# Sparse graph attention on one core: slot sums as accumulating float32 transposes, a count read one step later, and other FFN chunks

## The chip, the core and the metric

One Trainium2 chip, one of its eight cores. A core has five engines that run their own instruction streams in program order and meet at semaphores: TensorE (PE, with its weight loads PEld), VectorE (DVE), ScalarE (ACT), GpSimd (POOL) and SyncE (SP). DMA engines move data between the memory of the chip (HBM) and the on-chip memory (SBUF); TensorE writes its results to PSUM. The metric is the device time of the whole program in microseconds; less is better.

## What is computed

Four graph layers on 3327 nodes with 256 features, and an adjacency matrix in which an entry is set with probability 0.0048, some 16 neighbours for a node. Layer 0 is a one-head attention. Layers 1 to 3 are transformer layers with 8 heads of 32 features, in which a node attends to its neighbours only:

```python
def layer(x, adj, w_qkv, w_proj, b_proj, w1, b1, w2, b2, g1, be1, g2, be2):
    qkv = layer_norm(x, g1, be1) @ w_qkv              # float32 throughout
    q, k, v = split(qkv)                              # n x 8 heads x 32
    scores = einsum('nhd,mhd->hnm', q, k) * 32 ** -0.5
    scores = where(adj != 0, scores, -inf)
    attn = softmax(scores)
    out = einsum('hnm,mhd->nhd', attn, v).reshape(n, 256)
    x = x + out @ w_proj + b_proj
    ff = gelu(layer_norm(x, g2, be2) @ w1 + b1) @ w2 + b2      # 256 -> 1024 -> 256
    return x + ff
```

## The kernel before

Stage one computes layer 0 with dense products of the turned adjacency matrix. It also makes, for each node, the list of its neighbours, sorts the nodes by their number of neighbours and cuts them into 26 blocks of 128 nodes. A block `b` needs as many slots as its longest list has entries:

```python
CAPS = [40, 24, 22, 21, 20, 20, 19, 19, 18, 18, 17, 17, 17,
        16, 16, 15, 15, 15, 14, 14, 13, 13, 12, 12, 11, 10]      # 448 slots in all
GS = 4          # slots of one group: gathered into one buffer, worked on together
NBUF = 10       # such buffers
CB = 4          # blocks of one FFN chunk
```

A layer takes the blocks in the order 25, 1, 24, 2, ..., 13, 0. For each slot, POOL issues one gather that fetches the row with keys and values (512 numbers) of one neighbour for each of 128 nodes:

```python
for s in range(n):                                   # in issue(): n = 4 slots, or what is left
    nc.gpsimd.indirect_dma_start(out=t[:, s, :], in_=kv[L], in_offset=...neighbour s of block b...)
```

DVE multiplies the keys by the queries and sums over each head (`scores`, L1320 and L1321), and later multiplies the values by the softmax weights (L1361). PE then sums the slots: a product with the identity leaves each number as it is and PSUM adds it up. Slots are taken two at a time, so that even and odd slots land in two halves of a PSUM bank:

```python
nc.vector.tensor_mul(vw..., v, weights...)                                    # L1361
for s in range(0, n, 2):
    m = min(2, n - s) * D
    nc.tensor.matmul(self.po[b][:, :m], ident, vw[:, s * D:s * D + m],        # L1366
                     start=(s0 + s == 0), stop=(s0 + s + 2 >= S), skip_group_check=True)
self.issue()            # the buffer is free: gather the next group into it
```

When a block's slots are summed, a short list of steps is worked off, up to two steps in each turn; an empty step lets one half turn pass:

```python
def copy():    nc.scalar.copy(c["o"], self.po[b][:, :D])                      # L1384, even slots
def fold():    nc.vector.tensor_add(c["o"], c["o"], self.po[b][:, D:])        # L1387, + odd slots
def turn():                                                                   # L1391
    for k in range(2):
        nc.tensor.transpose(self.po[b][:, k * P:(k + 1) * P], c["o"][:, k * P:(k + 1) * P], ident)
def copy_T():  nc.scalar.copy(c["oT"], self.po[b][:, :2 * P])                 # L1396
def project(): ...  # bias (L1400) and c["oT"] @ w_proj (L1402), into the other half of po
def add():     ...  # x += po (L1406), and the moments for the norm
return [lambda: None, copy, lambda: None, fold, turn, copy_T, project, lambda: None, add]
```

Two blocks at most can own an accumulator `po` at a time. After the last block of a chunk, the norm, the FFN and (in layers 1 and 2) the next layer's q, k and v of these blocks become a long list of steps (`up` L1445, `gelu` L1451, `down` L1468, `back` L1482, `qkv` L1498), which is spread over the turns of the four blocks that follow. Every turn has one group's scores, one group's values and some of these steps.

In stage one, for every four blocks, a step `soft` marks the number of neighbours of each node (`OH`) and has PE count, with products of triangular matrices, the place of each node among the nodes with as many neighbours; DVE reads the count at once. A step `mix`, half a step of the pipeline later, finishes the weights of layer 0:

```python
def soft(self):
    nc.vector.tensor_tensor(OH[:, b0:b0 + n, :], ..., ALU.is_equal)           # L892
    for j in range(n):
        ...nc.tensor.matmul(at[:, j, :], lhsT, OH[:, m, :], ...)              # L903, 120 in all
    nc.vector.tensor_mul(t, at[:, :n, :], OH[:, b0:b0 + n, :])                # L906, waits for L903
    nc.vector.tensor_reduce(rank[:, b0:b0 + n], t, AX.X, ALU.add)
    ...                                # twelve small DVE steps and two exponentials on ACT
def mix(self):
    ...                                # ten DVE steps
```

Cuts are marked with `...`; the line numbers (L1366) are those of the kernel before.

Of the kernel before, what the change touches and what calls it, by code (L numbers as in the profile page):

```python
# [8 lines left out]
FP = mybir.dt.float32  # L9
# [3 lines left out]
ALU = mybir.AluOpType  # L13
AX = mybir.AxisListType
# [3 lines left out]
P = 128  # L18
N = 3327
D = 256  # L20
# [12 lines left out]
NB = (N + P - 1) // P  # L33
# [27 lines left out]
CB = 4  # L61
# [462 lines left out]
def sparse_path(ctx, tc, ins, out, dram, flag):  # L524
    nc = tc.nc
# [3 lines left out]
    ident = const.tile([P, P], FP, name="s_ident")  # L529
# [9 lines left out]
    rank = const.tile([P, NB], FP, name="rank")  # L539
# [83 lines left out]
    with tc.tile_pool(name="a", bufs=1) as a, tc.tile_pool(name="aw", bufs=2) as aw, \  # L623
# [44 lines left out]
        o = 0  # L668
        for name, n in (("gamma", D), ("beta", D), ("bt", H0), ("Wa", H0), ("ba", 1)):
# [10 lines left out]
        nd = LMAX + 1  # L680
# [3 lines left out]
        OH = a.tile([P, NB, nd], BF, name="OH")  # L684
        rest_tri = a.tile([P, P], BF, name="rest_tri")
        nc.vector.tensor_sub(rest_tri, ones_bf, tri)

        places = a_acc.tile([P, 512], FP, tag="places", name="places")
# [3 lines left out]
                         skip_group_check=True)  # L692
# [148 lines left out]
        class Group:  # L841
# [36 lines left out]
            def soft(self):  # L878


                g, n, b0 = self.g, self.n, self.blocks[0]

                def sv(name):
                    t = aw.tile([P, 4], FP, tag="s_" + name, bufs=1, name=f"s_{name}_{g}")
                    return t[:, :n]

                sg = S.s[:, b0:b0 + n]
                dg = deg[:, b0:b0 + n]
                nc.vector.tensor_copy(dg, self.acc[:, :n, H0])
                top = sv("top")  # L890
                nc.vector.tensor_scalar(top, dg, float(LMAX), None, ALU.min)
                nc.vector.tensor_tensor(OH[:, b0:b0 + n, :],  # L892
                                        num[:, None, :nd].to_broadcast([P, n, nd]),
                                        top[:, :, None].to_broadcast([P, n, nd]), ALU.is_equal)

                at = places[:, :4 * nd].rearrange("p (b k) -> p b k", k=nd)
                for j in range(n):
                    i = b0 + j
                    add = [(tri, i)] + [(ones_bf, k) for k in range(b0, i)]
                    if g:  # L900
                        add += [(rest_tri, i - 4)] + [(ones_bf, k) for k in range(i - 3, b0)]
                    for lhsT, m in add:
                        nc.tensor.matmul(at[:, j, :], lhsT, OH[:, m, :], start=False, stop=True,  # L903
                                         skip_group_check=True)
                t = aw.tile([P, 4, nd], FP, tag="place", bufs=1, name=f"place_{g}")[:, :n]
                nc.vector.tensor_mul(t, at[:, :n, :], OH[:, b0:b0 + n, :])  # L906
                nc.vector.tensor_reduce(rank[:, b0:b0 + n], t, AX.X, ALU.add)
                if b0 + n == NB:
                    nc.tensor.matmul(at[:, n - 1, :], rest_tri, OH[:, NB - 1, :], start=False,
                                     stop=True, skip_group_check=True)  # L910
                    S.all = at[:, n - 1, :]
                non, ga, fa, m1, m0, tt, mx = (
                    sv(k) for k in ("non", "ga", "fa", "m1", "m0", "tt", "mx"))
                nc.vector.tensor_scalar(non, dg, -1.0, float(N), ALU.mult, ALU.add)
                nc.vector.tensor_scalar(ga, dg, 0.0, None, ALU.is_gt)
                nc.vector.tensor_scalar(fa, non, 0.0, None, ALU.is_gt)
                nc.vector.tensor_scalar(tt, ga, -NEG0, NEG0, ALU.mult, ALU.add)
                nc.vector.tensor_mul(m1, sg, ga)
                nc.vector.tensor_add(m1, m1, tt)
                nc.vector.tensor_scalar(tt, fa, -1.0, 1.0, ALU.mult, ALU.add)  # L920
                nc.vector.tensor_mul(m0, sg, tt)
                nc.vector.scalar_tensor_tensor(m0, fa, NEG0, m0, ALU.mult, ALU.add)
                nc.vector.tensor_max(mx, m1, m0)
                nc.vector.tensor_sub(m1, m1, mx)
                nc.vector.tensor_sub(m0, m0, mx)
                nc.scalar.activation(m1, m1, AF.Exp)
                nc.scalar.activation(m0, m0, AF.Exp)
                self.non, self.m1, self.m0, self.tt = non, m1, m0, tt

            def mix(self):  # L930
                g, n, b0, acc = self.g, self.n, self.blocks[0], self.acc
                m1, m0, tt = self.m1, self.m0, self.tt
                z = aw.tile([P, 4], FP, tag="s_z", bufs=1, name=f"s_z_{g}")[:, :n]
                nc.vector.tensor_mul(z, deg[:, b0:b0 + n], m1)
                nc.vector.tensor_mul(tt, self.non, m0)
                nc.vector.tensor_add(z, z, tt)
                nc.vector.reciprocal(z, z)
                nc.vector.tensor_mul(m1, m1, z)
                nc.vector.tensor_mul(m0, m0, z)
                shape = [P, n, H0]  # L940
                nb = self.nb = aw.tile([P, 4, H0], FP, tag="nb", bufs=1, name=f"s_nb_{g}")[:, :n]
                t3 = aw.tile([P, 4, H0], FP, tag="t3", bufs=1, name=f"s_t3_{g}")[:, :n]
                nc.vector.tensor_sub(t3, S.hsum[:, None, :].to_broadcast(shape), acc[:, :n, :H0])
                nc.vector.tensor_mul(t3, t3, m0[:, :, None].to_broadcast(shape))
                nc.vector.tensor_mul(nb, acc[:, :n, :H0], m1[:, :, None].to_broadcast(shape))
                nc.vector.tensor_add(nb, nb, t3)

            def project(self):
                g, n = self.g, self.n
# [131 lines left out]
        for g in reversed(range(NG)):  # L1081
            at = dict(zip(names, (0, 1, 3, 4, 5, 6, 7, 8, 9, 10, 11, 12)))
# [11 lines left out]
            for name in names:  # L1094
                k = first + at[name]
# [39 lines left out]
        t = aw.tile([P, NB, nd], FP, tag="v", name="t_more")  # L1135
# [36 lines left out]
        for i in range(NB):  # L1172
            nc.tensor.matmul(pp[:, :2 * NB], oh_lo[:, i, :],
                             ids[:, i, :, :].rearrange("p a b -> p (a b)"),
                             start=(i == 0), stop=(i == NB - 1))
# [32 lines left out]
    work = ctx.enter_context(tc.tile_pool(name="b_work", bufs=2))  # L1208
# [53 lines left out]

    ORDER = [b for k in range(NB // 2) for b in (NB - 1 - k, k + 1)][:NB - 1] + [0]
    CHUNK, at = {}, 0
    for n in [CB - 1] + [CB] * ((NB - CB - 2) // CB) + [2, 1]:
        for b in ORDER[at:at + n]:
            CHUNK[b] = ORDER[at:at + n]
        at += n
# [3 lines left out]
    class Layer:  # L1272
# [77 lines left out]
        def values(self, b, s0):  # L1350

            L, S = self.L, CAPS[b]
            n = min(GS, S - s0)
            t = self.tiles.pop((b, s0))
            if s0 == 0:
                while len(self.po) > 1:
                    self.short.pop(0)()
                self.po[b] = ps_o.tile([P, 512], FP, tag="o", name=f"po_{L}_{b}")
            v = t[:, :n, D:2 * D].rearrange("p s (h d) -> p s h d", d=HD)
            vw = work.tile([P, GS * D], FP, tag="vw", bufs=3, name=f"vw_{L}_{b}_{s0}")  # L1360
            nc.vector.tensor_mul(  # L1361
                vw[:, :n * D].rearrange("p (s h d) -> p s h d", h=HEADS, d=HD), v,
                self.wp[b][:, s0:s0 + n, :, None].to_broadcast([P, n, HEADS, HD]))
            for s in range(0, n, 2):
                m = min(2, n - s) * D
                nc.tensor.matmul(self.po[b][:, :m], ident, vw[:, s * D:s * D + m],  # L1366
                                 start=(s0 + s == 0), stop=(s0 + s + 2 >= S),
                                 skip_group_check=True)
            self.issue()
            if s0 + GS >= S:  # L1370
                self.short += self.block(b)


        def block(self, b):
            L, w, c = self.L, self.w, {}
# [2 lines left out]
            if b == chunk[0]:  # L1378
                self.n2 = Norm(len(chunk), f"f{L}_{b}")
            n2 = self.n2  # L1380

            def copy():
                c["o"] = work.tile([P, D], FP, tag="o", name=f"o_{L}_{b}")
                nc.scalar.copy(c["o"], self.po[b][:, :D])  # L1384

            def fold():
                nc.vector.tensor_add(c["o"], c["o"], self.po[b][:, D:])  # L1387

            def turn():
                for k in range(2):  # L1390
                    nc.tensor.transpose(self.po[b][:, k * P:(k + 1) * P],  # L1391
                                        c["o"][:, k * P:(k + 1) * P], ident)

            def copy_T():
                c["oT"] = work.tile([P, 2 * P], FP, tag="oT", name=f"oT_{L}_{b}")
# [9 lines left out]
            def add():  # L1405
                nc.vector.tensor_add(x, x, self.po.pop(b)[:, D:])  # L1406
                n2.stats(chunk.index(b), x)
                if b == chunk[-1]:
# [3 lines left out]
                    turns = 5 if at == NB - 1 else turns - 2  # L1412
                    self.rate = sum(cost for cost, _ in self.long) / max(turns, 1)

            return [lambda: None, copy, lambda: None, fold, turn, copy_T, project, lambda: None, add]

        def chunk(self, blocks, n2):
            L, w, nxt = self.L, self.w, self.nxt
# [221 lines left out]
```

## Time and profile before

| what | value |
|---|---|
| time, median of 3 timed runs | 3311.32 us (3306.66 to 3313.2) |
| the profiled execution, first to last instruction | 2779.3 us |
| mean granted clock of TensorE in it | 0.836 |
| slot gathers on POOL (L1298) | 1344, 947 ns each, 1272.8 us |
| slot sums on PE (L1366) | 1380 records, 770.4 us |
| DVE on keys (L1320), head sums (L1321), values (L1361) | 413.3, 414.1 and 371.3 us |
| FFN products on PE (L1445, L1468) | 308.1 and 283.4 us |

The profile is of one execution; its span and the timed runs differ, and the page does not say by what. How to read its lines: busy time is the union of an engine's instructions. A group's row gives the line of the kernel, the engine, the operation, the output and the inputs, the shapes, how often it ran, then busy us and mean ns of one, then the idle time of the engine just ahead of these instructions and what ended it. Records of PE overlap, since a matmul starts while the one before it drains, so a group's busy time divided by its count is less than the mean of one. A float32 product shows as two records, each with its weight load. A row of the list of waits reads: who waited, for whom, us in total, times, the longest.

### The profile page before, as it was taken

How to read it: one execution, taken by the hardware profiler on the slowest of the kernel's cores; microseconds unless marked ns; L12 is line 12 of the kernel's file. 1: busy time of each engine (PE TensorE's matmuls, PEld its weight loads, DVE VectorE, ACT ScalarE, POOL GpSimd, SP SyncE). 2: the span in 40 equal slices, each digit the busy share in tenths (PEclk: the TensorE clock that was granted, in tenths of full speed). 3: DMA queues.
4: the chain of work that ended last, by engine and by line, in shares of the span. 5: the costliest groups of instructions: out<-in, count | busy, mean ns of one | idle time of the engine just before them, and what ended most of it. 6: DMA issues, size and time to landing. Idle time of an engine off the chain costs nothing. (4 is left out here: it accounts for less than half of the span.)

```text
span 2779.3 us, 21889 instructions
## 1 busy us (share of the span) xinstructions
PE 1952.0 (70%) x6409; PEld 1045.3 (38%) x6409; DVE 1961.9 (71%) x4061; ACT 806.5 (29%) x1398; POOL 1361.8 (49%) x1458
## 2 busy tenths in 40 slices
PE   5657665248788887884377887887853678867866
PEld 4546553114333333442133443433431333333334
DVE  6597888577877777733788677778427878778852
ACT  5346552102332322321022332232320222222221
POOL 4000000377766666601776565566017777776741
PEclk9768776678899898897788898898976898988988
DMA  6224420677766666613776565566227766666650
GB/s 235 99 106 154 155 81 32 198 217 217 222 196 200 202 182 186 182 34 100 209 211 201 168 195 180 158 190 178 50 70 210 210 183 199 201 190 184 198 130 15
DMA packets 144478, 453.66 MB, mean 163 GB/s; under 512 B 29521, under 2 KB 40156, under 8 KB 141021
## 3 DMA queue, kind: packets, MB, share of 16 engines
q0 software_dynamic: 113056, 370.26, 46.0%
q1 hardware_dynamic: 9834, 53.90, 5.5%
q10 hardware_dynamic: 21458, 28.02, 2.9%
q8 instruction: 52, 0.85, 0.1%
q14 instruction: 78, 0.64, 0.1%
HBM read 420.64 MB, written 31.42 MB: 163 GB/s over the span
## 5 line engine op out<-in xcount | busy, mean ns | idle before, releaser
L1298 POOL DMA_INDIRECT kv<-kv,t x1344 | 1272.8, 947 | 810.0 <-issue 350.4
L1366 PE MATMUL po<-vw,s_ident 128*128 128x512 f32 (+1 forms) x1380 | 770.4, 694 | 497.4 <-DVE vw L1361 447.6
L1320 DVE TENSOR_TENSOR kv<-kv,q 128x1024 f32<-128x1024 f32 (+3 forms) x363 | 413.3, 1139 | 312.6 <-ACT q L1306 156.5
L1366 PEld LDWEIGHTS po<-vw,s_ident 128*128 128x128 f32 x1380 | 285.3, 220 | 846.5 <-issue 468.3
L1321 DVE TENSOR_REDUCE sc<-kv 128x32 f32<-128x1024 f32 (+3 forms) x363 | 414.1, 1141 | 12.4
L1361 DVE TENSOR_TENSOR vw<-kv,w 128x1024 f32<-128x1024 f32 x333 | 371.3, 1127 | 0.2
L1445 PE MATMUL pu<-fT,s_w 128*128 128x512 f32 (+3 forms) x768 | 308.1, 536 | 1.0 <-ACT fT L596 1.0
L1468 PE MATMUL py<-gT,s_w 128*128 128x512 f32 (+2 forms) x672 | 283.4, 549 | 0.0
L1451 ACT ACTIVATE gT<-pu,pvb 128x512 f32<-128x512 f32 (+3 forms) x192 | 116.4, 607 | 361.0 <-PE pu L1445 360.7
L1445 PEld LDWEIGHTS pu<-fT,s_w 128*128 128x128 f32 x768 | 150.6, 206 | 140.5 <-issue 116.0
L711 POOL MEMSET s_abf<- 128x1 bf16 x23 | 2.2, 105 | 375.2 <-DVE s_v L731 248.3
L1468 PEld LDWEIGHTS py<-gT,s_w 128*128 128x128 f32 x672 | 127.6, 191 | 122.0 <-issue 104.4
L723 PE MATMUL s_ptb<-s_ident_bf,s_abf 128*128 128x128 bf16 x676 | 69.8, 273 | 77.3 <-ACT s_abf L714 64.0
L735 DVE MAX8 cand<-s_v 128x8 f32<-128x208 bf16 x416 | 118.0, 359 | 0.9
L588 ACT ACTIVATE xn_f<-t,nm_f,rqy_f 128x256 f32<-128x256 f32 x78 | 42.9, 593 | 247.5 <-DVE nm_f L582 240.1
L1498 PE MATMUL pk<-s_w_qkv,nT 128*128 128x512 f32 x208 | 104.4, 626 | 8.9 <-ACT nT L596 8.9
L1335 ACT ACTIVATE sc<-sc,mx 128x120 f32<-128x120 f32 (+6 forms) x78 | 32.0, 410 | 259.8 <-DVE mx L1332 259.2
L1406 DVE TENSOR_TENSOR t<-t,po 128x256 f32<-128x256 f32 x78 | 32.5, 417 | 103.8 <-PE po L1402 97.9
L1486 DVE TENSOR_TENSOR t<-t,pd 128x256 f32<-128x256 f32 x75 | 29.5, 408 | 91.0 <-PE pd L1482 91.0
L723 PEld LDWEIGHTS <-s_abf 128*128 128x128 bf16 x676 | 58.8, 125 | 91.8 <-ACT s_abf L714 70.8
L855 PE MATMUL s_pa<-s_aT,s_hs 128*128 128x256 bf16 x338 | 80.4, 286 | 13.2 <-DVE s_hs L817 13.2
L724 ACT COPY s_aT<-s_ptb 128x896 bf16<-128x896 bf16 x104 | 82.7, 859 | 19.9 <-PE s_ptb L723 19.7
(292 smaller groups left out, 2343.5 us busy)
## 6 DMA issues: line engine op xcount, KB each, us to landing
s_a<-in_adj_dram SPq DMA_DIRECT2D x25, 1663.5 KB
kv<-kv,t POOLq DMA_INDIRECT x1344, 3.7
kv<-kvr ACTq DMA_DIRECT2D x52, 256.0 KB
kv<-s_kvr ACTq DMA_DIRECT2D x26, 256.0 KB
s_w<-in_L_gnn_w_dram SPq DMA_DIRECT2D x6, 1024.0 KB
t<-ql ACTq DMA_DIRECT2D x6, 592.0 KB
t<-s_x ACTq DMA_DIRECT2D x6, 512.0 KB
s_w_qkv<-in_L_gnn_w_qkv_dram SPq DMA_DIRECT2D x3, 768.0 KB
```

Source lines behind the costliest of these rows:

```text
L723: nc.tensor.transpose(pt[:, m, :], self.abf[:, k * P:(k + 1) * P], ident_bf)
L724: nc.scalar.copy(aT[:, k0:k0 + len(ks), :], pt[:, :len(ks), :])
L735: nc.vector.max(out=self.cand[:, s, :], in_=self.v[:, s, :])
L1298: nc.gpsimd.indirect_dma_start(out=t[:, s, :], out_offset=None, in_=kv[L], in_offset=bass.IndirectOffsetOnAxis(ap=t2[:, b, k:k + 1].bitcas ...
L1320: nc.vector.tensor_mul(k, k, self.q[b][:, None, :].to_broadcast([P, n, D]))
L1321: nc.vector.tensor_reduce(self.sc[b][:, s0:s0 + n, :], k.rearrange("p s (h d) -> p s h d", d=HD), AX.X, ALU.add)
L1361: nc.vector.tensor_mul(vw[:, :n * D].rearrange("p (s h d) -> p s h d", h=HEADS, d=HD), v, self.wp[b][:, s0:s0 + n, :, None].to_broadcast([ ...
L1366: nc.tensor.matmul(self.po[b][:, :m], ident, vw[:, s * D:s * D + m], start=(s0 + s == 0), stop=(s0 + s + 2 >= S), skip_group_check=True)
L1445: nc.tensor.matmul(c["pu", f][:, :n], w["w1"][:, e, f * P:(f + 1) * P], c["hT"][:, e, :n], start=(e == 0), stop=(e == 1))
L1451: nc.scalar.activation(g[:, :n], c.pop(("pu", f))[:, :n], AF.Gelu_apprx_tanh, bias=w["b1"][:, f:f + 1])
L1468: nc.tensor.matmul(c["py"][e][:, :n], w["w2"][:, f, e * P:(e + 1) * P], g[:, :n], start=(f == 0), stop=last)
L1498: nc.tensor.matmul(ps[:, :c1 - c0], c["hT"][:, e, j * P:(j + 1) * P], nxt["w_qkv"][:, e, c0:c1], start=(e == 0), stop=(e == 1))
```

## The change

It has three parts. The slot sums become transposes: each half of a slot's 256 numbers is the stationary operand and the identity the moving one, in PE's transpose mode, and the transposes of all slots of a block add up in the same PSUM columns. The sum so comes out transposed, as the projection wants it, and the steps `copy`, `fold` and `turn` go. The count of places is read at the end of `mix` instead of in `soft`, so that PE has longer to make it. And the first FFN chunk of a layer, of three blocks, becomes one of one block and one of two, so that FFN work starts earlier.

```diff
                     for lhsT, m in add:
                         nc.tensor.matmul(at[:, j, :], lhsT, OH[:, m, :], start=False, stop=True,
                                          skip_group_check=True)
-                t = aw.tile([P, 4, nd], FP, tag="place", bufs=1, name=f"place_{g}")[:, :n]
-                nc.vector.tensor_mul(t, at[:, :n, :], OH[:, b0:b0 + n, :])
-                nc.vector.tensor_reduce(rank[:, b0:b0 + n], t, AX.X, ALU.add)
-                if b0 + n == NB:
-                    ...                       # one more product for the last group
...
+            def place(self):
+                ...                           # the lines above, unchanged
...  # end of mix
                 nc.vector.tensor_add(nb, nb, t3)
+                self.place()
...
-    for n in [CB - 1] + [CB] * ((NB - CB - 2) // CB) + [2, 1]:
+    for n in [1, 2] + [CB] * ((NB - CB - 2) // CB) + [2, 1]:
         for b in ORDER[at:at + n]:
             CHUNK[b] = ORDER[at:at + n]
...
-            for s in range(0, n, 2):
-                m = min(2, n - s) * D
-                nc.tensor.matmul(self.po[b][:, :m], ident, vw[:, s * D:s * D + m],
-                                 start=(s0 + s == 0), stop=(s0 + s + 2 >= S),
-                                 skip_group_check=True)
+            for s in range(n):
+                for k in range(2):
+                    at = s * D + k * P
+                    nc.tensor.matmul(self.po[b][:, k * P:(k + 1) * P], vw[:, at:at + P], ident,
+                                     is_transpose=True, start=(s0 + s == 0 and k == 0),
+                                     stop=(s0 + s + 1 == S), skip_group_check=True)
             self.issue()
...
-            def copy():                       # and fold() and turn(), as above
-                ...
-            return [lambda: None, copy, lambda: None, fold, turn, copy_T, project, lambda: None, add]
+            return [lambda: None, copy_T, project, lambda: None, add]
```

More of the change, by code (lines that the diff above doesn't have):

```diff
@@ L904, in soft @@
                                          skip_group_check=True)
-                t = aw.tile([P, 4, nd], FP, tag="place", bufs=1, name=f"place_{g}")[:, :n]
-                nc.vector.tensor_mul(t, at[:, :n, :], OH[:, b0:b0 + n, :])
-                nc.vector.tensor_reduce(rank[:, b0:b0 + n], t, AX.X, ALU.add)
-                if b0 + n == NB:
-                    nc.tensor.matmul(at[:, n - 1, :], rest_tri, OH[:, NB - 1, :], start=False,
-                                     stop=True, skip_group_check=True)
-                    S.all = at[:, n - 1, :]
                 non, ga, fa, m1, m0, tt, mx = (
@@ L928, in soft @@
                 self.non, self.m1, self.m0, self.tt = non, m1, m0, tt
+            def place(self):
+                g, n, b0 = self.g, self.n, self.blocks[0]
+                at = places[:, :4 * nd].rearrange("p (b k) -> p b k", k=nd)
+                t = aw.tile([P, 4, nd], FP, tag="place", bufs=1, name=f"place_{g}")[:, :n]
+                nc.vector.tensor_mul(t, at[:, :n, :], OH[:, b0:b0 + n, :])
+                nc.vector.tensor_reduce(rank[:, b0:b0 + n], t, AX.X, ALU.add)
+                if b0 + n == NB:
+                    nc.tensor.matmul(at[:, n - 1, :], rest_tri, OH[:, NB - 1, :], start=False,
+                                     stop=True, skip_group_check=True)
+                    S.all = at[:, n - 1, :]
             def mix(self):
@@ L1380, in block @@
             n2 = self.n2
-            def copy():
[L1383 to L1392, printed above, removed]
             def copy_T():
```

## The prediction

> **What bounds the kernel now.** I read the busy shares first, then a table of stages, then the gathers by stage, then the waits. The first line of the page names no single bound:
>
> ```profile
> PE 1952.0 (70%) x6409; PEld 1045.3 (38%) x6409; DVE 1961.9 (71%) x4061; ACT 806.5 (29%) x1398; POOL 1361.8 (49%) x1458
> ```
>
> A first stage (layer 0, lists, ranking) ends at 525 us, where the first neighbour gather starts. Three equal attention layers follow. The first and last gathers of the layers start at 525.0 and 1179.7, 1303.5 and 1952.5, 2074.6 and 2683.3 us. I cut the layers there and asked for busy times; columns are the window, its length, then busy us (instructions) of PE, weight loads, DVE, ACT, POOL, then granted clock, DMA share, GB/s:
>
> ```profile
> 800.00:1150.00 350.00, 284.37 (x730) 135.19 (x728) 262.78 (x464) 110.82 (x240) 216.90 (x230) 0.90 0.65 189
> 1150.00:1305.00 155.00, 114.33 (x352) 64.54 (x352) 64.42 (x158) 43.45 (x90) 24.82 (x26) 0.88 0.28 78
> 1500.00:1950.00 450.00, 371.45 (x950) 175.80 (x949) 338.80 (x578) 133.36 (x226) 277.99 (x295) 0.89 0.61 180
> 2200.00:2640.00 440.00, 344.64 (x864) 159.76 (x863) 347.25 (x528) 113.48 (x185) 317.33 (x333) 0.89 0.65 193
> ```
>
> In mid-layer PE is busy 81 to 83% and DVE 75 to 79%; both run in program order and hand work to each other, so each one's rest is a wait for the other. POOL is the hard floor behind them: a gather takes 0.947 us and the next starts 0.30 us later, 1.247 us each, so the 448 gathers of a layer need 559 us. They take 655, 649 and 609. In layer 1 POOL also issues 26 row gathers and in layer 3 26 stores (about 33 us each time), so the slack above POOL's floor is about 63, 90 and 17 us, 170 us in all: the most that a faster PE and DVE can recover in mid-layer. Why POOL pauses is in the list of waits:
>
> ```profile
> DVE kv L1320 <- ACT q L1306: 156.5, 42, 7.3
> ACT o L1384 <- PE po L1366: 117.5, 20, 21.3
> POOL kv L1298 <- DVE vw L1361: 102.4, 43, 9.4
> DVE t L1406 <- PE po L1402: 97.9, 36, 6.6
> DVE place L906 <- PE places L903: 41.1, 7, 16.2
> DVE o L1387 <- ACT o L1384: 39.0, 13, 12.3
> ```
>
> POOL waits for the ring slot that DVE's weighted product frees; DVE waits for ACT's copy of q; ACT, in order too, is stuck behind copies that wait for PE. So PE sets the pace from behind. After each layer's last gather come 124, 122 and 96 us of drain, PE busy about 74% of it.
>
> **What the Trainium skill says.** "FP8 and Floating Point Precision", TensorE Precision Notes: a true float32 product takes four passes through the array. "Perfetto Trace Analysis", Transposes: a transpose has a path that skips arithmetic. The trace agrees with both together: a float32 product shows as two records, each of 0.43 us for 512 columns, and a transpose as one:
>
> ```profile
> 2708.05 1.88 PE L1366 MATMUL po<-vw,s_ident 128*128 128x512 f32 x4
> 2709.77 1.04 PE L1482 MATMUL pd<-s_ident,yT 128*128 128x128 f32 x8
> ```
>
> The first four run until the next starts: 1.72 us, 0.43 each. Eight transposes take 1.04 us with the last one's 0.273 us of latency, so (1.04 - 0.273)/7 = 0.110 us each, weight load included.
> "PSUM — Partial Sum Buffer", The four PSUM rules: a float32 transpose sets the bits that make a later one add; no transpose accumulates in this trace, so that rests on the page. "TensorE: Matmul & The Clock Gate", Part 4, says that transposes don't keep the clock up. Here the trace disagrees: at 105.1 us PE did 26 transposes and nothing else, and the clock rose for the next window (PE busy is the second figure, the clock third from the end):
>
> ```profile
> 105.10:108.50 3.40, 2.87 (x26) 2.64 (x27) 3.03 (x6) 2.19 (x4) 0.00 (x0) 0.50 0.67 200
> 108.50:112.00 3.50, 3.50 (x35) 3.33 (x34) 3.38 (x13) 3.50 (x3) 0.10 (x1) 0.99 0.72 297
> ```
>
> So I don't expect the change to force the half clock; a PE with more gaps will merely see it more often (0.90 becomes 0.8, a guess).
>
> **The slot sums.** Before, these forms on PE:
>
> ```profile
> L1366 PE MATMUL po<-vw,s_ident 128*128 128x512 f32 x1308 | 752.9, 711 | 497.4 <-DVE vw L1361 447.6 <-DVE rqv_f L551 49.3
> L1391 PE MATMUL po<-s_ident,o 128*128 128x128 f32 x156 | 33.3, 298 | 18.4 <-DVE o L1387 18.4
> L1366 PE MATMUL po<-vw,s_ident 128*128 128x256 f32 x72 | 21.9, 386 | 0.0
> ```
>
> At full clock: 1308 x 0.43 + 72 x 0.215 = 578 us. After: 448 slots x 3 layers x 2 = 2688 transposes x 0.11 = 296 us. The result is already transposed, so the 156 transposes of L1391 go too (17 us). PE saves 578 + 17 - 296 = 299 us at full clock, at the mid-layer clock of 0.9 some 330 us of its 1952. ACT loses the copy at L1384 (78 x 0.368 = 29 us), DVE the fold at L1387 (78 x 0.415 = 32 us) and its 39 us of wait. The short list of a block falls from nine entries to five, so its place in the accumulator comes free two turns sooner. Added: four times the weight loads for these sums (inside the 0.110), and loads that now wait for DVE's product, where the identity could be loaded ahead: 0.14 us a group, mostly off the path.
>
> What of it reaches the end? At POOL's pace of 80 gathers in 100 us, mid-layer PE would need about: now 82 busy at 66 gathers, of which 66/4 x 1.72/0.9 = 31.5 are sums; other work 50.5 x 80/66 = 61; sums 20 x 0.88/0.85 = 21; together 82. DVE: 75 x 80/66 = 91, less 2 for the fold. POOL 100. Three engines near full in lockstep don't reach the floor of the fullest, so I take 55% of the 170 us: **95 us**. In the drains, about ten buffered groups x 0.84 us and three turns of copy, fold and transpose (about 1.2 us each): 12 us x 3 = **36 us**.
>
> **The count of places.** DVE stood 41.1 us in seven waits at L906, the longest 16.2, because PE had the turned adjacency and a run of sums ahead of the count. DVE is busy 378 of the first 483 us and paces that stage. Reading the count in the next half step puts a list (about 3.5 us: two steps of 0.29, five maxima of 0.295 and four replacements of 0.37) and some 4 us of small steps before it; short waits vanish, the longest keeps half. I take **25 us**.
>
> **FFN chunks.** 3, 4, ... becomes 1, 2, 4, ...: the first FFN starts two blocks sooner, when PE is busy under half the time (43.5 of 115 us at 1305:1420). It brings one block's FFN, some 32 records of 0.21 us, forward into idle time. It costs an extra chain of about 13 small DVE steps (2.2 us) for each of five norms, 11 us of DVE, and 8 x (0.367 + 0.473 - 0.580) = 2.1 us of ACT a layer. I count **0**, give or take 15.
>
> Sum in the profiled execution: 95 + 36 + 25 = 156 us of 2779, 5.6%.
>
> **From profile to time.** The timed runs are 3311 us where the profiled execution is 2781; the page doesn't say where the 530 us are. If they are the same in both kernels: 3311 - 156 = 3155. If everything stretches alike: 3311 x 0.944 = 3125. If PE alone is slower there, its weight grows: 330 us of PE work become 400 and more, and about 2950 is possible. If gathers alone are slower there, the gain is hidden in mid-layer: only stage one and drains, about 3250. I say 3130.
>
> **Rivals.** (1) POOL becomes the bound at once: layer 3 already runs at 75 gathers in 100 us and DVE waits there for arriving gathers. For it: 17 us of slack there. Against it: 90 in layer 2. It would give 2779 - 60, timed about 3230. (2) DVE takes over: 91% at POOL's pace, with the new norms; the waits on PE then turn into busy DVE and the gain is half, timed about 3210. (3) PE pays more than 0.110 us a transpose, since each needs its own weights, or falls to half clock between sparse bursts: 2688 x 0.22 = 591 us, no saving at all; only the removed copy, fold and turn are left, about 3260. The eight-in-a-row above speaks against it. (4) PE was the only pacer and the timed runs are PE-bound throughout: 2950.
>
> **Range and chances.** 2980 to 3230 covers full recovery with a slow PE down to a POOL bound. Slower by 2% would need transposes at twice their measured cost and more: 0.03. Within 2% (above 3245) is rival 3 or a gather-bound timed run: 0.10.
>
> **What would show it.** L1366 with 2688 records of 128x128 and spacing 0.11 us; PE busy near 1620 us; no L1384, L1387, L1391 work; gathers of the layers spanning about 615, 600, 600 us; the wait of DVE for places under 12 us and the first gather near 500. Wrong would be: gather spans unchanged (PE wasn't the pacer), PE busy unchanged (transposes cost double), or a time that moves far more than the profiled span (the timed runs have another bound).

## The result, and the profile after

In the set of runs that gave the time of the kernel before, the changed kernel takes **3164.92 us** (median of 4, 3155.03 to 3169.98) against 3310.58 us (median of 4, 3306.66 to 3313.2): a ratio of 0.9557, 95% interval 0.9532 to 0.9583. The prediction was 3130 us in a range of 2980 to 3230.

In that first set both kernels ran slower than in every later one, where the kernel before took 2767 to 2791 us (medians 2779 to 2783), which is the span of its profile, and the changed one 2564.66 us (median of 4, 2563.6 to 2565.33; ratio 0.9232, 0.9212 to 0.9252). So the change is worth 145.7 us in the first set and 215.6 us in a later one. The 530 us between profile and time, which the prediction could not place, belonged to the set and not to the kernel; what differed in that set is not known.

The profile after that came with the first set shows what such a run looks like. From its list of waits (who waited, for whom, us in total, times, the longest):

```profile
POOL kv L1303 <- issue: 563.2, 1167, 18.5
ACT gT L1445 <- remote: 411.7, 34, 30.6
POOL kv L1303 <- DVE vw L1366: 366.3, 65, 17.7
...
PE po L1372 <- issue: 212.2, 87, 35.0
```

"remote" is a releaser that the trace does not know, and "issue" is time in which the engine waited for nothing that the trace shows. One such stall, from the timeline of PE (start, us, engine, line; idle before in brackets):

```profile
608.66 1.09 PE L1372 MATMUL po<-s_ident,vw 128*128 128x128 f32 x8 [0.66 <-issue]
635.25 1.22 PE L1439 MATMUL pu<-fT,s_w 128*128 128x128 f32 x4 [25.50 <-issue]
```

and the same moment on ACT:

```profile
634.83 0.37 ACT L1445 ACTIVATE gT<-pu,pvb 128x128 f32<-128x128 f32 x1 [30.64 <-remote]
```

For 25.5 us PE does nothing and ACT waits for it, 30.6 us, with no reason in the record. What holds PE there was not found; no later run showed it, so no experiment could change it. From here on I read the profile of the same kernel, unchanged, from a later set. Its expectation uses results of the parts, which stand further below.

> The changed kernel, unchanged, on the chip on which its parts were taken. If the parts add (sums 2589.8, count -23.2, chunks +1.5, beside a before of 2783.3): 2568 us, ratio 0.923, and no waits put down to an unknown releaser. If the 0.956 first measured is a property of the kernel: 2660 us.

Its span is 2561.8 us. First line of its page, as the busy shares of before:

```profile
PE 1677.4 (65%) x7702; PEld 1142.8 (45%) x7702; DVE 1947.9 (76%) x4048; ACT 806.2 (31%) x1364; POOL 1362.0 (53%) x1458
```

The first of the two came: 2564.66 us, and no wait is put down to an unknown releaser. PE fell by some 274 us, DVE by 14; POOL has the same work in less time. The stages of its layers (window, length, busy us of PE, weight loads, DVE, ACT, POOL, then clock, DMA share, GB/s). The first, third and fourth lie inside the gathers of layers 1, 2 and 3, the second is the drain of layer 1:

```profile
779.00:1103.00 324.00, 253.28 (x975) 153.31 (x974) 269.15 (x463) 112.25 (x233) 238.41 (x253) 0.84 0.77 219
1103.00:1201.00 98.00, 64.15 (x279) 46.89 (x279) 41.11 (x113) 29.11 (x60) 0.94 (x2) 0.82 0.24 67
1388.00:1792.00 404.00, 319.52 (x1241) 194.12 (x1239) 335.68 (x567) 134.97 (x215) 283.25 (x300) 0.85 0.70 204
2115.00:2460.00 345.00, 225.88 (x862) 136.80 (x862) 268.33 (x408) 85.04 (x129) 249.73 (x264) 0.79 0.67 194
```

In layers 1 and 2 DVE now has a larger busy share than PE, 83% (269.15 of 324, 335.68 of 404) against 78 and 79%; before, PE led. POOL's share looks smaller than it is, since the 0.30 us from one gather to the next don't count as busy: at the prediction's 1.247 us for each of its instructions POOL is taken up for 97, 93 and 95% of the three gather windows (253, 300 and 264 instructions), where it was 82, 82 and 94% before. So POOL is the fullest now. The gathers move 219 and 204 GB/s where it was 189 and 180. The waits:

```profile
POOL kv L1303 <- issue: 333.5, 1089, 1.6
...
DVE kv L1325 <- DMA kv<-kv,t: 138.0, 83, 7.2
DVE kv L1325 <- ACT q L1311: 105.5, 36, 7.1
...
POOL kv L1303 <- DVE vw L1366: 42.0, 35, 3.1
```

POOL's wait for a ring slot fell from 102.4 us to 42.0 us, its longest from 9.4 to 3.1. Nearly all of it lies in layer 2, 97.5 us before and 37.7 after. In layer 1, before, POOL's pauses stand mostly under ACT's copy L1384 (22.0 us in 3 waits) and under "issue" (151.9 us in 371 waits, where 0.30 us each would make 111); after, "issue" is 115.1 us in 372. DVE's wait for the copy of q fell from 156.5 us (144.1 when the kernel before was repeated) to 105.5 us. The rows of ACT's copy L1384, DVE's fold L1387 and PE's turn L1391 are gone. ACT's wait for PE is shorter and not gone: it was 117.5 us at the first copy and 124.4 at the second, L1396, and at the one copy that is left it is

```profile
ACT oT L1390 <- PE po L1372: 182.5, 64, 21.1
```

DVE's largest wait for an operand in the scores is the arriving gathers, as it already was in the repeat of the kernel before (152.8 us there). The sums themselves, by form:

```profile
L1372 PE MATMUL po<-s_ident,vw 128*128 128x128 f32 x2688 | 450.6, 325 | 468.0 <-DVE vw L1366 466.5
```

450.6 us where the two forms had 774.8, and nearly all of the idle time ahead of them is a wait for DVE's product: PE works off a burst and waits for the next one. A burst of 48 in the timeline of PE gives the spacing:

```profile
1164.37 5.72 PE L1372 MATMUL po<-s_ident,vw 128*128 128x128 f32 x48
```

(5.72 - 0.273)/47 = 0.116 us.

To put the saving in its place I repeated the kernel before as well and took the times of the first and last gather of each layer from both traces. A span runs from the first to the last gather of a layer, a drain from the last one to the next layer's first, or to the end.

> The kernel before, unchanged, for its profile beside the others. Theory A (the 2779 us profile and the 3311 us times are two ways in which the same program runs): this profile shows a span near 3310 us, and in it waits put down to no known releaser and idle times of TensorE of 15 to 30 us, as in the profile after (ACT at the gelu: 411.7 us put down to 'remote'). Theory B (the profile of before is typical, and the timed runs have something outside the span): span near 2780 us again, time near 3310.

Neither came: span and time are both near 2775 us, so there is nothing outside the span, and no wait inside it is put down to an unknown releaser.

| us | start of gathers | span 1 | span 2 | span 3 | drain 1 | drain 2 | drain 3 |
|---|---|---|---|---|---|---|---|
| before (profiled span 2773.7, time 2775.45) | 522.9 | 647.1 | 650.4 | 608.2 | 126.2 | 122.2 | 96.7 |
| after (profiled span 2561.8, time 2563.6) | 503.9 | 599.3 | 591.0 | 604.0 | 97.8 | 98.5 | 67.3 |
| gain | 19.0 | 47.8 | 59.4 | 4.2 | 28.4 | 23.7 | 29.4 |

The gains add up to 211.9 us: 19.0 in stage one, 111.4 in mid-layer, 81.5 in the drains.

### The profile page after: what moved, and what is told of

Its sections match the earlier page's. It is cut to its first block, busy times and chain, and to the rows that moved or that the text cites. A ratio compares the mean times of both kernels' runs of the same rounds, so it can differ in the third digit from the quotient of the medians.

```text
span 3168.1 us, 24437 instructions
## 1 busy us (share of the span) xinstructions
PE 1790.0 (57%) x7702; PEld 1182.8 (37%) x7702; DVE 1946.3 (61%) x4048; ACT 801.1 (25%) x1364; POOL 1361.6 (43%) x1458
## 4 chain that ended last, share of the span: by engine, by line
issue 14%; PE 11%; POOL 11%; DVE 11%; another core or an unknown queue 9%; DMA 3%; ACT 2%; DVEq 0%; POOLq 0%; ACTq 0%; SPq 0%
POOL kv L1303 11%; PE pu L1439 3%; DVE kv L1325 3%; DMA kv<-kv,t 3%; DVE vw L1366 2%; PE po L1372 2%; PE py L1462 2%; DVE sc L1326 2%; PE pk L1492 2%; PE pq L1492 1%; PE po L1396 0%; PE pf L591 0%; ACT gT L1445 0%; DVE t L1480 0%
## 5 line engine op out<-in xcount | busy, mean ns | idle before, releaser
L1372 PE MATMUL po<-s_ident,vw 128*128 128x128 f32 x2688 | 473.5, 333 | 517.0 <-DVE vw L1366 302.2
L1372 PEld LDWEIGHTS po<-s_ident,vw 128*128 128x128 f32 x2688 | 391.0, 173 | 651.0 <-issue 363.5
L1439 PE MATMUL pu<-fT,s_w 128*128 128x512 f32 (+2 forms) x864 | 353.9, 546 | 174.0 <-issue 72.5
L1366 DVE TENSOR_TENSOR vw<-kv,w 128x1024 f32<-128x1024 f32 x333 | 371.4, 1128 | 92.9 <-remote 84.7
L1462 PE MATMUL py<-gT,s_w 128*128 128x512 f32 (+1 forms) x672 | 306.9, 578 | 42.1 <-issue 34.5
L1439 PEld LDWEIGHTS pu<-fT,s_w 128*128 128x128 f32 x864 | 177.2, 227 | 304.7 <-issue 180.3
L1445 ACT ACTIVATE gT<-pu,pvb 128x512 f32<-128x512 f32 (+2 forms) x216 | 121.5, 568 | 661.5 <-remote 411.7
L1396 PEld LDWEIGHTS po<-s_w_proj,oT 128*128 128x128 f32 x312 | 68.3, 243 | 181.2 <-issue 171.8
L1390 ACT COPY oT<-po 128x256 f32<-128x256 f32 x78 | 28.9, 371 | 388.1 <-remote 170.5
L1396 PE MATMUL po<-s_w_proj,oT 128*128 128x256 f32 x312 | 105.5, 472 | 0.0
L591 PE MATMUL pf<-s_ident,xn_f 128*128 128x128 f32 x156 | 45.4, 434 | 103.1 <-ACT xn_f L588 76.8
L1480 DVE TENSOR_TENSOR t<-t,pd 128x256 f32<-128x256 f32 x72 | 28.3, 404 | 108.1 <-PE pd L1476 80.6
```

Of the source, the lines that this page charges most:

```text
L1366: nc.vector.tensor_mul(vw[:, :n * D].rearrange("p (s h d) -> p s h d", h=HEADS, d=HD), v, self.wp[b][:, s0:s0 + n, :, None].to_broadcast([ ...
L1372: nc.tensor.matmul(self.po[b][:, k * P:(k + 1) * P], vw[:, at:at + P], ident, is_transpose=True, start=(s0 + s == 0 and k == 0), stop=(s0 ...
L1396: nc.tensor.matmul(ps, c["oT"][:, k * P:(k + 1) * P], w["w_proj"][:, k, :], start=False, stop=(k == 1))
L1439: nc.tensor.matmul(c["pu", f][:, :n], w["w1"][:, e, f * P:(f + 1) * P], c["hT"][:, e, :n], start=(e == 0), stop=(e == 1))
L1445: nc.scalar.activation(g[:, :n], c.pop(("pu", f))[:, :n], AF.Gelu_apprx_tanh, bias=w["b1"][:, f:f + 1])
L1462: nc.tensor.matmul(c["py"][e][:, :n], w["w2"][:, f, e * P:(e + 1) * P], g[:, :n], start=(f == 0), stop=last)
```

## The experiments

**The parts alone.** Theory: the slot sums bring nearly everything, because PE had set the pace; the count brings stage one; the chunks bring nothing. Rival: the chunks start FFN work earlier and carry a good part of the gain. Three kernels, each with one part of the change. Their expectations still count from the 3311 us of the first set, so it is the differences that can be compared.

Sums only:

```diff
+            for s in range(n):
+                for k in range(2):
+                    at = s * D + k * P
+                    nc.tensor.matmul(self.po[b][:, k * P:(k + 1) * P], vw[:, at:at + P], ident,
+                                     is_transpose=True, ...)
...
-            return [lambda: None, copy, lambda: None, fold, turn, copy_T, project, lambda: None, add]
+            return [lambda: None, copy_T, project, lambda: None, add]
```

> Only the slot sums as accumulating transposes, with copy, fold and turn gone; count of places and chunks as before. If the sums carry the gain, as predicted (131 of 156 us): 3185 us, ratio 0.962. If the hand-offs between engines set the time and not TensorE's busy time, the three removed steps a block still help, but less: 3250 us.

Count of places only:

```diff
-                nc.vector.tensor_mul(t, at[:, :n, :], OH[:, b0:b0 + n, :])     # in soft
+                self.place()                                                   # at the end of mix
```

> Only the count of places read in mix. Prediction: 25 us less (3285), with DVE's wait at the count from 41 to under 12 us and the first gather near 500 us. Rival: the stage waits on something else and 0 to 10 us come of it.

Chunks only:

```diff
-    for n in [CB - 1] + [CB] * ((NB - CB - 2) // CB) + [2, 1]:
+    for n in [1, 2] + [CB] * ((NB - CB - 2) // CB) + [2, 1]:
```

> Only the FFN chunks of 1, 2, 4, ... in place of 3, 4, .... Prediction: no change, give or take 15 us (3295 to 3325). Rival: the extra norm and 96 more up-records and their hand-offs cost more than the early start brings, 20 to 40 us more; or the opposite sign, since the last chunk of a layer meets less backlog.

| kernel | us | ratio to before, 95% interval |
|---|---|---|
| before | 2783.27 | |
| sums only | 2589.75 | 0.9313 (0.9296 to 0.933) |
| count only | 2760.04 | 0.9918 (0.9902 to 0.9935) |
| chunks only | 2784.76 | 1.0002 (0.9986 to 1.0017) |

193.5, 23.2 and -1.5 us. The sum, 215.2, is the 215.6 us of the whole: within the few us that the runs scatter, the parts don't lean on each other. The count did what it was for. DVE's waits for places, before:

```profile
DVE place L906 <- PE places L903: 38.7, 7, 15.0
```

and with the count alone moved:

```profile
DVE place L927 <- PE places L903: 6.5, 2, 3.9
```

The first gather then starts at 504.1 us where it was 522.9. That the chunks are worth nothing holds beside the other parts too: a kernel with the sums and the count, but the chunks of before, takes the same time as the whole change.

> Sums and count, chunks as before. If the chunks are worth nothing beside the other parts too: equal to the whole change within 5 us. If they help once TensorE is no longer behind: the whole change is 10 to 30 us faster than this; if their extra norm hurts once DVE is fuller: 10 us slower.

Measured 2566.64 us, ratio 0.9237 (0.9216 to 0.9257), against 0.9232 (0.9212 to 0.9252) for the whole.

**Mode or steps?** The new sums do two things at once: each slot costs PE less, and three steps (copy, fold, turn) vanish behind a block. To part them, the same products with the same operands and the same shorter list, but without the transpose mode, as true float32 products:

```diff
-                                     is_transpose=True, start=(s0 + s == 0 and k == 0),
+                                     start=(s0 + s == 0 and k == 0),
```

> As the sums alone, but without transpose mode: the same operands as a true float32 product, which sums the same numbers into the same places. TensorE's work for the sums is then what it was (2688 products of two records of 128 columns, about 0.107 us each at full clock: 575 us), while copy, fold and turn stay away. Theory A (TensorE's time in the sums was the pace): 2720 to 2770 us, near the kernel before. Theory B (the three steps and their hand-offs were the pace): 2600 to 2640, near the sums alone.

2701.55 us, ratio 0.9722 (0.9701 to 0.9744): between the two theories, so each has a part of the truth. PE is as busy as before, 1958.4 us where it was 1951.4. So the vanished steps and the turned result bring 78.7 us with no saving on PE, and the mode the other 112 us (2701.55 to 2589.75; the two come from different sets, whose kernels before differ by 3 us). The sums in this kernel, by form:

```profile
L1367 PE MATMUL po<-s_ident,vw 128*128 128x128 f32 x5376 | 779.9, 310 | 373.2 <-DVE vw L1361 373.1
```

Two records for each product, 5376 for 2688, and 779.9 us, as costly as the sums before. The same row in the kernel with the sums only:

```profile
L1367 PE MATMUL po<-s_ident,vw 128*128 128x128 f32 x2688 | 453.9, 327 | 498.2 <-DVE vw L1361 496.9
```

One record each and 326 us less. POOL's wait for its ring slot follows: 86.3 us with true products against 102.8 before,

```profile
POOL kv L1298 <- DVE vw L1361: 86.3, 41, 6.1
```

and 43.1 with transposes:

```profile
POOL kv L1298 <- DVE vw L1361: 43.1, 39, 3.7
```

By stages, from the gathers: the removed steps take 10.7, 18.0 and -1.3 us off the three spans and 15.1, 10.4 and 22.2 off the three drains; the mode takes another 37.2, 41.4 and -0.4 off the spans and 13.3, 13.3 and 7.8 off the drains. The mode works in mid-layer, where PE's busy time counts; the steps work mainly in the drains, where I take the length of a chain to count. What the kernel with true products changes besides the steps (operands that change places, an accumulator that comes free sooner) no run parts from them.

**How much is left in the sums?** If PE still paced the layers, cutting the sums further would go on paying; if POOL had become the bound (the first rival), it would not. The kernel with the sums only, in which just the first slot of every group of four is summed. The other slots' sums are left out, so the output is not the reference's; gathers, scores and products are all there:

```diff
-            for s in range(n):
+            for s in range(1):
...
-                                     stop=(s0 + s + 1 == S), skip_group_check=True)
+                                     stop=(s0 + GS >= S), skip_group_check=True)
```

> As the sums alone, but only the first slot of each group of four is transposed into the sum; the other slots' sums are left out, so the output is not the reference's. TensorE loses three quarters of the sums (some 220 us at full clock). If GpSimd's gathers are the bound in mid-layer after the change: gather spans of the layers stay at 592 to 600, 585 and 610 us, and only the drains lose 3 to 8 us each, 2570 us. If TensorE still sets the pace: the spans fall by another 20 us or more each, 2500 us.

2548.71 us in one run. The row of the sums:

```profile
L1367 PE MATMUL po<-s_ident,vw 128*128 128x128 f32 x726 | 186.5, 354 | 642.7 <-DVE vw L1361 642.5
```

267 us of PE's busy time went, and the program gained 41 us, between the two expectations. The first step of the same kind, true products to transposes, took away 326 us and gained 112. The spans are now 589.1, 572.8 and 609.0 us, against floors of POOL, by the prediction's count of 1.247 us a gather plus 33 us of other issues in layers 1 and 3, of 592, 559 and 592. Layer 1 is at its floor, within what the estimate is good for, and layer 2 is 14 us above it; there POOL still waits 18.5 us for ring slots. Layer 3 did not move in any of these kernels, and the waits of POOL inside its span say why. Before:

```profile
POOL out_dram L1511 <- DMA out_dram<-t,perm: 14.5, 6, 4.0
```

and in the kernel with a quarter of the sums:

```profile
POOL out_dram L1500 <- DMA out_dram<-t,perm: 26.0, 10, 6.7
POOL out_dram L1500 <- issue: 2.7, 9, 0.3
```

Only 19 of the 26 stores of results fall inside the span. In the second kernel they take 20.4 us and POOL stands 28.7 us before them, mostly for the transfer of a store before; with 448 gathers at 1.247 us, 559 us, that is 608 of the 609.0 us. Before, where some of these waits ended with DVE, POOL stood 29.0 us in all, which makes 608 of 608.8. So the gathers of layer 3 come one right behind the other in both, and what lies above them is POOL's own stores. Taking away three quarters of the sums did not shorten them.

**The drain.** 81.5 us of gain where 36 were expected made the drains worth a look. In the timeline of DVE of the changed kernel, in the drain of layer 1:

```profile
1150.76 0.42 DVE L1480 TENSOR_TENSOR t<-t,pd 128x256 f32<-128x256 f32 x1 [15.92 <-PE pd L1476]
...
1155.34 3.49 DVE L1366 TENSOR_TENSOR vw<-kv,sc 128x1024 f32<-128x1024 f32 x3
...
1165.44 3.49 DVE L1366 TENSOR_TENSOR vw<-kv,sc 128x1024 f32<-128x1024 f32 x3 [5.18 <-PE po L1372]
```

DVE stands 15.92 us at the end of an FFN chunk, and behind it, in program order, wait the weighted values of seven of the last block's ten groups (L1366), which need nothing from that chunk. Three variants of the changed kernel move this: the FFN steps of the chunk before last spread over ten turns and not five; a last chunk of three blocks; three last chunks of one.

```diff
-                    turns = 5 if at == NB - 1 else turns - 2
+                    turns = 10 if at == NB - 1 else turns - 2
```

> A try at a better version: the changed kernel, but the two-block FFN chunk before the last block is spread over 10 turns in place of 5. In the drain of layer 1 DVE stands 15.9 us at the second residual sum (waiting for TensorE's FFN) while the last block's weighted values wait behind it in DVE's order. If that order costs the time: drains 98, 98 and 67 become 88 to 92 and 60, 2540 us. If the two FFN chains only change places: same within 8 us.

```diff
-    for n in [1, 2] + [CB] * ((NB - CB - 2) // CB) + [2, 1]:
+    for n in [1, 2] + [CB] * ((NB - CB - 2) // CB) + [3]:
```

> The changed kernel with the last two chunks (of two blocks and of one) as one of three: one chain of norm, FFN, norm and projection after the last gather in place of two. If the number of chains sets the drain: 10 to 15 us less in each of three layers, 2530 us. If the work of two blocks that the other order hides behind the last block's ten groups counts for more: drains 10 us longer, 2595 us.

```diff
-    for n in [1, 2] + [CB] * ((NB - CB - 2) // CB) + [2, 1]:
+    for n in [1, 2] + [CB] * ((NB - CB - 2) // CB) + [1, 1, 1]:
```

> The changed kernel with the last chunks 1, 1, 1 in place of 2, 1: the first of the two FFNs starts a block earlier, hidden behind the gathers, and a single one is left in front of the last. If the drain is FFN work: 6 to 10 us less in each, 2540 us. If the extra norm and smaller products cost as much: the same.

| kernel | us | ratio to before, 95% interval | drains 1, 2, 3 |
|---|---|---|---|
| changed kernel | 2564.66 | 0.9232 (0.9212 to 0.9252) | 97.8, 98.5, 67.3 |
| ten turns | 2565.78 | 0.9228 (0.9204 to 0.9252) | 93.7, 91.5, 78.3 |
| last chunk of 3 | 2571.93 | 0.925 (0.9228 to 0.9273) | 92.1, 96.0, 81.4 |
| last chunks 1, 1, 1 | 2596.63 | 0.9332 (0.9308 to 0.9357) | 107.8, 108.6, 74.5 |

Ten turns take the same time as the changed kernel, a last chunk of three 7 us more, and none of the three does what either expectation of it said. Both of the first two shorten the drains of layers 1 and 2 and lose that in the last one; that this is because layer 3 has no q, k and v of a next layer was not tested. Chunks of one are worse in every drain. So ten turns where a next layer follows and five at the end:

```diff
-                    turns = 5 if at == NB - 1 else turns - 2
+                    turns = (10 if self.nxt is not None else 5) if at == NB - 1 else turns - 2
```

> The changed kernel with the last two-block FFN chunk spread over 10 turns in layers 1 and 2 only, where that shortened the drains (97.8 and 98.5 to 93.7 and 91.5 us), and over 5 in layer 3, where it made the end 11 us later. If the layers' drains are independent: 11 us less than the changed kernel, 2554 us, ratio 0.919. If the gain was chance of one profile: 2565.

2554.86 us (2552.99 to 2560.92), ratio 0.9201 (0.9176 to 0.9227), drains 93.8, 92.3 and 67.8: the quickest of all that computes the whole. In its trace the values that wait behind L1480 in the drain of layer 1 start 46.3 us after the last gather, where it was 52.1; the wait itself is hardly shorter, 14.5 us, but it starts earlier. Its lead on the changed kernel is some 10 us: the runs of the two don't overlap, but they come from different sets, and the intervals of their ratios do. The drains of its trace are 9.7 us shorter in sum, and those of layers 1 and 2 come out as in the kernel with ten turns everywhere. The lead is likely, then, and not settled.

## Why the prediction was right, and where it was not

**The time.** 3130 was 1.1% below 3164.92, but the way there holds two misses that cancel. In the sum of 156 us the gain was too small: 215.6 us were measured in a later set. And "if they are the same in both kernels", said of the 530 us between profile and time, is not what happened: they were 530.3 us for before (3310.58 - 2780.27) and 600.3 for the changed kernel (3164.92 - 2564.66). 70 us of the gain went under the conditions of the first set, whose cause stays open. That 3130 came so near is in good part luck.

**PE as the pacer: right.** With the sums alone the gathers of layers 1 and 2 take 599 and 591 us where they took 647 and 650. Taking the transpose mode out again, which changes PE's work and nothing of DVE or POOL, gave most of that back: 636 and 632. Mid-layer gained 111.4 us, 95 predicted: 65% of the 170 us that the prediction saw above POOL's floor, not 55%. The 17 us of layer 3 among them were not PE's to give, as POOL spends them at its stores. The guessed clock of 0.8 is 0.84 and 0.85 in layers 1 and 2 and 0.79 in layer 3; it fell from 0.89 as PE had more gaps, and with a quarter of the sums it fell further (0.738 over the run, 0.775 with all of them). The Trainium skill, "TensorE: Matmul & The Clock Gate", Part 4, says that transposes don't keep the clock up. A mean of 0.84 says little on that, since PE does true products in between, but one stretch has nothing else on PE than 16 of these transposes:

```profile
1261.93 3.64 PE L1372 MATMUL po<-s_ident,vw 128*128 128x128 f32 x16 [6.26 <-DVE vw L1366]
```

and the clock rises behind it from 0.50 to 1.00, so here too the trace disagrees:

```profile
1262.02:1265.43 3.41, 3.41 (x16) 3.15 (x16) 3.34 (x6) 0.34 (x2) 2.70 (x3) 0.50 0.70 202
1265.43:1268.85 3.42, 2.12 (x17) 1.80 (x16) 3.39 (x4) 2.32 (x5) 2.60 (x3) 1.00 0.70 213
```

**PE's saving: right in kind, too large.** 0.110 us a transpose held (0.116 in a burst of 48), but of the 330 us 274 were saved. The row of the sums fell by 774.8 - 450.6 = 324 us and the turn's by 33. Other work of PE took longer. The mean clock is lower, 0.786 where it was 0.834, and the unchanged projection (L1402 before, L1396 after), 312 records, rose from 82.9 to 96.9 us of busy time; the clock granted at the starts of its records fell from a mean of 0.98 to 0.88, which by the ratio of the two makes some 9 of these 14 us (an estimate). The new chunks add 96 records to the FFN's first product as well (303.4 us before, 330.4 after, 320.2 with the sums only).

**The drains: the term that was mis-sized.** 36 us predicted, 81.5 measured. The groups were not far off: "about ten buffered groups x 0.84 us" is 25 us for three layers, and the mode took 34.4 us off the drains. The failed step is "three turns of copy, fold and transpose (about 1.2 us each)", 10.8 us for three layers: the kernel with true products shows 47.7 us for it, 10 to 22 us a drain. The 1.2 us is the work of one such step. But an entry of the list is half a turn, and in a drain a turn also carries steps of the FFN and the norms, on which DVE waits up to 15.9 us. That this is why a turn is so dear is argued from the timeline; no run changed the length of a turn alone.

**The count: right.** 25 us predicted, 23.2 measured alone, of which the start of the gathers shows 18.8 (522.9 to 504.1); the wait is under 12 us (6.5), the first gather near 500 (504).

**The chunks: right.** 0 give or take 15; -1.5 us alone, 2.0 us beside the rest.

**Readings that were a little off.** In layer 3 PE was busy 78% (344.64 of 440) and not 81; gathers came there at 72 in 100 us and not at 75, since 17 of the 333 instructions of POOL were stores; and in the drains alone PE was busy 71, 72 and 66%, not 74. None of these carries the sum.

**The rivals.** POOL as the bound at once (first): wrong as a whole, since layer 2 was free to gain 59 us, but right for layer 3. The 4 us that it gained came with the chunks (609.8 us with the sums and the count, 604.0 with the chunks too). And it is now nearly true in layer 1, 599 us with a floor of 592. DVE as the bound (second): it is at 83% and not at the 91% that I feared, for the gathers of layers 1 and 2 come at 75 and 74 in 100 us and not at 80. Transposes at twice the cost (third): wrong, though the kernel with true products shows what that rival describes, a gain from the removed steps alone; it is 79 us, where the rival had put some 50. "PE was the only pacer" (fourth): wrong, since the fewer sums pay less and less, 112 us for 326 and then 41 for 267.

## What to carry to other kernels

When a product with the identity only adds up slots, ask whether the next step wants the result turned: the transpose mode does both, in one record of 128 columns where a true product showed two, and the copy, the addition and the turn behind it go. In a drain, price a removed step by the length of the chain that it stood in, with everything its turn carries, and not by its own duration. Before a profile and a timed run are set against each other, repeat the unchanged kernel in the set that is to be compared: a gap between the two may belong to neither kernel.

## What the runs showed that I had not expected

That a transpose would add float32 numbers more cheaply than a product was the ground of the prediction. How cleanly it can be seen was new: with the same operands, the same shape and the same accumulators, 2688 products cost PE 779.9 us and 2688 transposes 453.9 us. A weight load for every 128 columns did not show in PE's busy time: the true products with the old operands, one identity against 512 columns, had cost the same 778 us (756.5 + 21.4). And the three steps behind each block, which the prediction priced by their own work at 10.8 us for the three drains, gave 47.7 us there and 79 us of the program.
